# Self-attention over four images: first image's projection with its bias added on TensorE and one unit of lead, projection steps four ahead, column sums in a free PSUM bank, operands 64 bytes apart

## The chip, the cores and the metric

One core of a Trainium2 chip. TensorE (PE) multiplies, reading both operands from SBUF and writing sums into PSUM, which has eight banks of 128 x 512 float32 here. ScalarE (ACT), VectorE (DVE) and GpSimd (POOL) work beside it; SyncE (SP) and POOL issue most of the DMAs. Every engine works through its own queue in order, and semaphores hold an instruction back until what it reads or overwrites is ready. The metric is device time in microseconds (us) of one execution; lower is better.

## The reference

For each of four images, x has 4096 positions of 256 channels:

```
q = x @ Wq + bq          # 4096 x 128
k = x @ Wk + bk          # 4096 x 128
v = x @ Wv + bv          # 4096 x 256
pq, pk, pv = q, k, v reshaped to (-1, 4096)   # rows 128, 128, 256
energy = pq.T @ pk                            # 4096 x 4096
attention = softmax(energy, axis=-1)
out = pv @ attention.T                        # 256 x 4096, reshaped back
result = gamma * out + x                      # float32
```

## The kernel before, in words

**Number forms.** A float32 is kept as a shortened high part h and two combinations with the rest, so that products of the short type float32r add up to float32 accuracy. "Forms 0, 1, 2" are these three tensors: h is made by ACT (line 202 for x, 248 for q and k, 153 for v and the weights, 322 for the exponentials), the other two by DVE (204 and 206, 251, 156, 336 and 338). A product is built in one PSUM bank: first the products with form 2, then the partial sum is scaled in place (the "seed"), then the products with forms 0 and 1 are added on top.

**Projection.** An image has 16 units of 256 positions. One unit is: four transposes of x on PE (`transposed`, line 191), the forms of x (`x_forms`), q and k together (`products(b, i, 0, ...)`: 4 products of 128x256 with form 2, then 8 with forms 0 and 1), v (`products(b, i, 1, ...)`, likewise). Between the two parts stands the seed: for q and k on DVE, which scales by REST and adds the bias (`seed_qk`, line 233); for v on ACT, in two halves, with the bias as a column (`seed_v`, line 240). Then come the forms of the results; those of q and k go to DRAM in four stores of 192 KB on POOL's queue (`store`, line 270), from a tile with two buffers (`pf`). Image 0's v stays in SBUF (`vall`), the later images' v goes through DRAM as well.

Image 0 is projected alone ahead of everything (loop at line 527). In each iteration PE's order is: transposes of unit i+1, form-2 products of q/k of unit i, form-2 products of v, the rest of q/k, the rest of v. The first three query and key tiles are loaded in units 6 to 8 (lines 560 to 563), and the first two attention steps' scores are made in units 12 to 15. Six PSUM banks go round for all of it (line 515).

**Attention.** For each image there are 8 groups of 512 queries (g), and for each group 16 steps (t) of 256 keys: 128 steps an image, 512 in all (loop at line 567, n counts them). One step holds `cross` (2 products of 128x512 and ACT's scaling, lines 298 and 299), `energy` (4 products and ACT's exponentials, lines 313 and 316), both for two steps ahead (LOOK); `upper` (ACT's h of the exponentials); `halves` (DVE: running column sums at line 331 and the two other forms, for one step ahead); and `attend`, 12 products in two halves j of 6, into four PSUM banks a0, b0, a1, b1 (line 355). So a step has 18 products of 512 columns on PE. Into these steps the next image's projection is worked: `step(n, engine)` gives one eighth of a unit's work to each engine's place in a step (line 467), a unit in 8 steps, with r = step modulo 8 (0: transposes; 1 and 2: forms of x; 3: form-2 products of q/k and seed; 4: the rest of q/k; 5 and 6: v; 7 and 0: its forms). It uses two PSUM banks ("p", twice).

**Change of group.** At t = 15 and the following t = 0 the four banks are emptied into SBUF by ACT (`emptied`, line 369; j = 0 at t = 15, j = 1 at t = 0), and the column sums of the softmax are added over the partitions by two products with ones (`sum_forms`, lines 378 and 379, and `sums`, line 384), into bank b1 once that is emptied. ACT copies one row of it (line 385), and `finish` takes that row through DRAM to reciprocals, scales the group's output, adds x and stores it, some piece in each following step.

ACT's order around the change is: at t = 15 scalings, sum form, projection, exponentials, emptying j = 0, `upper`; at t = 0 scalings, emptying j = 1, projection, exponentials, the copy of the sums, `upper`. PE's order: at t = 15 `cross`, `attend` j = 0, `energy`, projection, `attend` j = 1; at t = 0 `cross`, `attend` j = 0, `energy`, `sums`, projection, `attend` j = 1. DVE makes its part of the sum form ahead of `halves`.

Of the kernel before, what the change touches and what calls it, by code (L numbers as in the profile page):

```python
# [20 lines left out]
def kernel(  # L21
# [36 lines left out]
    nc = tc.nc  # L58
# [42 lines left out]
    with ExitStack() as fast:  # L101
# [10 lines left out]
        ps_p = pool("ps_p", 2, space=PSUM)  # L112
# [4 lines left out]
        wf = qkv.tile([P, 2, 3, KC, C], F32R, tag="wf", name="wf")  # L117
# [8 lines left out]
        nc.gpsimd.memset(zs, 1.0)  # L126
        make_identity(nc, ident)
# [5 lines left out]
        nc.gpsimd.dma_start(gam, gamma.partition_broadcast(P))  # L133
        nc.gpsimd.dma_start(bias[:, :C2], bq.partition_broadcast(P))
        nc.gpsimd.dma_start(bias[:, C2:], bk.partition_broadcast(P))
        for eh in range(KC):
            nc.gpsimd.dma_start(bvs[:, eh : eh + 1], bv[eh * P : (eh + 1) * P].unsqueeze(1))
        nc.gpsimd.tensor_scalar(bias, bias, REST, None, ALU.mult)
# [20 lines left out]
        def weights(w):  # L159

            nc.scalar.mul(scaled[:, w], raw[:, w], E ** -(w + 1))
            yield from split(*(wf[:, w, f] for f in range(3)), scaled[:, w])
# [23 lines left out]
        def transposed(b, i):  # L186
            xs = loads.pop(("x", b, i))
            tp = units["xt", b, i] = bank(f"xt_{b}_{i}", [P, KC, 2, P])
            for k in range(KC):
                for s in range(2):  # L190
                    nc.tensor.transpose(tp[:, k, s, :], xs[:, s, k * P : (k + 1) * P], ident)  # L191

        def x_forms(b, i):

            y = units.pop(("xt", b, i))
            if b == 0:
                f = ppool.tile([P, 3, KC, 2, P], F32R, tag="ld", name=f"xf_{b}_{i}")
            else:
                f = work.tile([P, 3, KC, 2, P], F32R, tag="xf", name=f"xf_{b}_{i}", bufs=1)
            units["xf", b, i] = f  # L200
            h = f[:, 0]
            nc.scalar.activation(h, y, AF.Identity, scale=UPPER)  # L202
            yield
            nc.vector.scalar_tensor_tensor(f[:, 2], h.bitcast(F32), 1.0 + E, y, ALU.mult, ALU.subtract)
            yield
            nc.vector.tensor_tensor(f[:, 1], y, h.bitcast(F32), ALU.subtract)
            yield

        def products(b, i, w, fs):

            xf = units["xf", b, i]
            if fs[0] == 2:
                units[w, b, i] = bank(f"qv{w}_{b}_{i}", [P, 2, C])
            to = units[w, b, i]
            for f in fs:
                for s in range(2):
                    for k in range(KC):
                        if w:
                            left, right = wf[:, 1, f, k, s * P : (s + 1) * P], xf[:, f, k]
                        else:  # L220
                            left, right = xf[:, f, k, s, :], wf[:, 0, f, k]
                        nc.tensor.matmul(  # L222
                            to[:, s, :],
                            left,
                            right.rearrange("p s a -> p (s a)") if w else right,
                            start=(f == 2 and s == k == 0),
                            stop=(f == 1 and k == KC - 1),
                            skip_group_check=True,
                        )

        def seed_qk(b, i):
            y = units[0, b, i]
            nc.vector.scalar_tensor_tensor(  # L233
                y, y, REST, bias.unsqueeze(1).to_broadcast([P, 2, C]), ALU.mult, ALU.add
            )
# [137 lines left out]
        def sum_forms(n):  # L373

            s = now["total"] = now["sum"]
            f = work.tile([P, 2, NB], F32R, tag="r", name=f"zf_{n // NU}", bufs=1)
            h, l = now["z"] = f[:, 0, :], f[:, 1, :]
            nc.scalar.activation(h, s[:, 0, :], AF.Identity, scale=UPPER)  # L378
            nc.vector.tensor_tensor(l, s[:, 0, :], h.bitcast(F32), ALU.subtract)

        def sums(n):
            zp = ps_o.tile([P, NB], F32, tag="b1", name=f"z_{n // NU}")
            for f, x in enumerate(now["z"]):
                nc.tensor.matmul(zp, ones_r, x, start=(f == 0), stop=(f == 1))  # L384
            nc.scalar.copy(now["total"][0:1, 0, :], zp[0:1, :])  # L385
# [35 lines left out]
        def finish_last(n, xr):  # L421
# [26 lines left out]
            np_ = ps_p.tile([P, 1], F32, tag="p", name="np")  # L448
# [18 lines left out]
        def step(n, engine):  # L467
# [47 lines left out]
        now["banks"] = cycle(  # L515
            [(ps_o, "a0"), (ps_o, "a1"), (ps_o, "b0"), (ps_o, "b1"), (ps_p, "p"), (ps_p, "p")]
        )
        image(0)
        for i in range(3):
            load_x(0, i)  # L520
        transposed(0, 0)
        first = [weights(0), x_forms(0, 0), weights(1)]
        for pieces in first + [first[0], first[1], first[2]]:
            next(pieces)
        for pieces in first:
            next(pieces)
        for i in range(NI):
            load_x(0, i + 3)
            if i + 1 < NI:
                transposed(0, i + 1)  # L530
                xs = x_forms(0, i + 1)
            else:
                xs = iter(())
            products(0, i, 0, (2,))
            seed_qk(0, i)
            products(0, i, 1, (2,))
            next(xs, None)
            seed_v(0, i)
            if i in (12, 14):
                cross(i // 2 - 6)  # L540
# [4 lines left out]
            if i in (12, 14):  # L545
                energy(i // 2 - 6)
            vs = v_forms(0, i)
            next(vs)
            for _ in xs:
                pass  # L550
            for _ in qk:
                pass
            for _ in vs:
                pass
            store()
            if i in (13, 15):
                upper(i // 2 - 6)
            if i == 14:
# [5 lines left out]
            if i in (13, 15):  # L564
                load_k(i // 2 - 3)
        now["banks"] = cycle([(ps_p, "p")])
        for n in range(B * STEPS):
# [3 lines left out]
            if u == 0 and b + 1 < B:  # L571
                image(b + 1)
                load_x(b + 1, 0)
# [26 lines left out]
            attend(n, 1)  # L600
            if t == 6 and n + NU < B * STEPS:
# [221 lines left out]
```

## Time and profile before

| | |
|---|---|
| time, median of 3 runs | 2421.97 us (2421.1 to 2422.91) |
| the profiled execution | 2424.35 us, span 2422.6 us, granted clock 0.994 |
| busy: PE / DVE / ACT / POOL | 2358.6 / 2138.0 / 1870.8 / 581.7 us |
| projection of image 0 | from 0 to about 101 us, a unit from start to start mostly 5.03 us |
| a group of 16 steps with projection | 73.8 us (PE busy 73.2) |
| a group of 16 steps of the last image | 67.0 us |
| DMA moved | 413.8 MB, 170 GB/s of HBM traffic over the span |

The span runs from the first to the last instruction; the execution's time has some 1.75 us more around it. Busy times overlap between engines. PE's busy time includes the modelled end of each matmul, which overlaps the next one's start, so short waits of PE can lie hidden in it; distances from start to start show them. "Idle before" of an instruction is the time its engine did nothing, with the instruction that ended it. L233 is line 233 of the kernel.

### The profile page before, as it was taken

How to read it: one execution, taken by the hardware profiler on the slowest of the kernel's cores; microseconds unless marked ns; L12 is line 12 of the kernel's file. 1: busy time of each engine (PE TensorE's matmuls, PEld its weight loads, DVE VectorE, ACT ScalarE, POOL GpSimd, SP SyncE). 2: the span in 40 equal slices, each digit the busy share in tenths (PEclk: the TensorE clock that was granted, in tenths of full speed). 3: DMA queues.
4: the chain of work that ended last, by engine and by line, in shares of the span. 5: the costliest groups of instructions: out<-in, count | busy, mean ns of one | idle time of the engine just before them, and what ended most of it. 6: DMA issues, size and time to landing. Idle time of an engine off the chain costs nothing.

```text
span 2422.6 us, 31905 instructions
## 1 busy us (share of the span) xinstructions
PE 2358.6 (97%) x11094; PEld 1954.4 (81%) x11094; DVE 2138.0 (88%) x2126; ACT 1870.8 (77%) x3076; POOL 581.7 (24%) x943
## 2 busy tenths in 40 slices
PE   6799999999999999999999999999999999999998
PEld 6688888888888888888888888888888888888886
DVE  7789988889989899888899898898888888888887
ACT  4577777877877877778778778778777778787875
POOL 5422222222322222212233122222123111111110
PEclk9999999999999999999999999999999999999999
DMA  9756655656796666566699566675569644444443
GB/s 200 169 143 166 180 143 158 177 156 181 217 296 171 168 164 181 146 158 178 157 284 265 147 165 166 170 181 147 154 176 315 198 127 131 120 119 125 120 123 92
DMA packets 243990, 413.82 MB, mean 171 GB/s; under 512 B 26031, under 2 KB 141487, under 8 KB 243822
## 3 DMA queue, kind: packets, MB, share of 16 engines
q0 software_dynamic: 203152, 368.77, 57.2%
q1 hardware_dynamic: 40126, 42.67, 6.4%
q8 instruction: 91, 1.49, 0.3%
q14 instruction: 77, 0.63, 0.1%
q10 hardware_dynamic: 544, 0.26, 0.0%
HBM read 306.64 MB, written 104.98 MB: 170 GB/s over the span
## 4 chain that ended last, share of the span: by engine, by line
PE 86%; ACT 9%; DMA 2%; DVE 1%; issue 1%; POOL 0%; SPq 0%; DVEq 0%; ACTq 0%
PE a L355 35%; PE b L355 17%; PE e L313 17%; PE e L298 9%; PE qv L222 7%; ACT o L369 3%; ACT e L299 2%; ACT x L316 1%; ACT h L322 1%; PE z L384 1%; PE xt L191 1%; DMA k<-kf 1%; DMA qd<-f 1%; ACT zf L378 1%; DVE v L156 0%
## 5 line engine op out<-in xcount | busy, mean ns | idle before, releaser
L316 ACT ACTIVATE x<-e 128x512 f32<-128x512 f32 x960 | 523.8, 600 | 319.1 <-PE e L313 316.0
L285 POOL DMA_DIRECT2D k<-kf x512 | 275.8, 539 | 1743.3 <-PE e L313 1638.6
L331 DVE TENSOR_TENSOR s<-s,x 128x1024 f32<-128x1024 f32 x480 | 585.8, 1220 | 95.1 <-ACT x L316 92.7
L299 ACT ACTIVATE e<-e 128x512 f32<-128x512 f32 x1024 | 547.4, 574 | 137.2 <-PE e L298 136.5
L355 PE MATMUL a<-h,v 128*128 128x512 f32 x2048 | 640.0, 394 | 0.0
L355 PE MATMUL a<-ld,v 128*128 128x512 f32 x2048 | 633.4, 390 | 0.0
L355 PE MATMUL b<-ld,v 128*128 128x512 f32 x2048 | 631.7, 390 | 0.0
L336 DVE TENSOR_TENSOR ld<-x,h 128x1024 fp32r<-128x1024 f32 x480 | 585.4, 1220 | 30.9 <-PE b L355 24.8
L338 DVE SCALAR_TENSOR_TENSOR ld<-h,x 128x1024 fp32r<-128x1024 f32 x480 | 584.4, 1218 | 0.0
L313 PE MATMUL e<-q,k 128*128 128x512 f32 x2048 | 552.0, 391 | 4.5
L322 ACT ACTIVATE h<-x 128x1024 fp32r<-128x1024 f32 x480 | 509.9, 1062 | 13.3
L313 PEld LDWEIGHTS e<-q,k 128*128 128x128 f32 x2048 | 379.4, 188 | 98.1 <-ACT e L299 23.2
L355 PEld LDWEIGHTS a<-ld,v 128*128 128x128 f32 x2048 | 385.1, 188 | 83.2
L355 PEld LDWEIGHTS b<-ld,v 128*128 128x128 f32 x2048 | 383.9, 188 | 82.8 <-ACT s L385 1.4
L355 PEld LDWEIGHTS a<-h,v 128*128 128x128 f32 x2048 | 369.3, 189 | 62.7 <-issue 1.0
L298 PE MATMUL e<-q,k 128*128 128x512 f32 x1024 | 316.3, 390 | 0.6 <-DMA k<-kf 0.6
L298 PEld LDWEIGHTS e<-q,k 128*128 128x128 f32 x1024 | 192.0, 188 | 42.3 <-issue 1.6
L222 PE MATMUL qv<-wf,xf 128*128 128x256 f32 x768 | 117.6, 290 | 26.0 <-DVE qv L233 25.9
L222 PEld LDWEIGHTS qv<-wf,xf 128*128 128x128 f32 x768 | 109.1, 194 | 37.4 <-DVE qv L233 29.5
L222 PEld LDWEIGHTS qv<-xf,wf 128*128 128x128 f32 x768 | 108.8, 193 | 7.5
L222 PE MATMUL qv<-xf,wf 128*128 128x256 f32 x768 | 113.9, 285 | 0.0
L270 POOL DMA_DIRECT2D kf<-f x128 | 98.4, 769 | 41.0 <-ACT xf L202 20.6
(79 smaller groups left out, 1215.1 us busy)
## 6 DMA issues: line engine op xcount, KB each, us to landing
k<-kf POOLq DMA_DIRECT2D x512, 384.0 KB, 3.5
vf<-vf POOLq DMA_DIRECT2D x48, 768.0 KB, 6.0
v<-vf POOLq DMA_DIRECT2D x48, 768.0 KB, 7.2
kf<-f POOLq DMA_DIRECT2D x128, 192.0 KB, 3.4
qd<-f POOLq DMA_DIRECT2D x128, 192.0 KB, 3.1
q<-qd POOLq DMA_DIRECT2D x32, 768.0 KB, 4.7
o<-in_x_dram POOLq DMA_DIRECT2D x31, 512.0 KB, 7.7
out_dram<-o SPq DMA_DIRECT2D x31, 512.0 KB
```

The source lines that it names most:

```text
L222: nc.tensor.matmul(to[:, s, :], left, right.rearrange("p s a -> p (s a)") if w else right, start=(f == 2 and s == k == 0), stop=(f == 1 an ...
L270: nc.gpsimd.dma_start(to, f)
L285: nc.gpsimd.dma_start(t, kf[b, u % NU])
L298: nc.tensor.matmul(e, *forms(n, i, 2), start=True, stop=False, skip_group_check=True)
L299: nc.scalar.mul(e, e, -REST)
L313: nc.tensor.matmul(e, *forms(n, i, f), start=False, stop=(f == 1), skip_group_check=True)
L316: nc.scalar.activation(x[:, i, :], e, AF.Exp, scale=(1.0 + E) ** 3 / E)
L322: nc.scalar.activation(h, units[n], AF.Identity, scale=UPPER)
L331: nc.vector.tensor_tensor(s, s, x, ALU.add)
L336: nc.vector.tensor_tensor(l, x, h.bitcast(F32), ALU.subtract)
L338: nc.vector.scalar_tensor_tensor(d, h.bitcast(F32), 1.0 + E, x, ALU.mult, ALU.subtract)
L355: nc.tensor.matmul(to, vall[:, t, f, i, j * P : (j + 1) * P], units[n][f][:, i, :], start=(t == 0 and i == 0 and f != 1), stop=(t == NU - ...
```

## The change

- **Image 0's bias by PE.** q's and k's bias is split into two forms `bf`, divided by 128 (one made by ACT, one by DVE); four products of 128x256 with a matrix of ones add it into the bank behind the form-2 products (`biased`). The seed for image 0 is then a scaling alone, on ACT. The bias copies are issued first on POOL, gamma's last; POOL's scaling of `bias` for the later images moves behind the weights' forms.
- **A unit of lead.** In each iteration PE's order is: the rest of q/k of unit i, the rest of v, transposes of unit i+2, form-2 products and bias of q/k of unit i+1, form-2 products of v. Transposes alternate between the two p banks, products go round the four others. The loads of queries and keys move to units 4 to 6 (then 8 and 11), the first two steps' scores to units 7 to 12, `halves(0)` stays in unit 14.
- **Steps four ahead.** The projection's step is p = n for n < 8, two steps in each of n = 8 to 11, then p = n + 4. The next image's tiles and its first load are prepared five steps ahead of the image's end.
- **Change of group.** `sums` uses a p bank and stands behind the projection's products. At t = 15 `emptied` j = 0 stands where `upper` stood; `upper` follows at t = 0 behind the scalings; `emptied` j = 1 moves behind the exponentials of t = 0. DVE's part of the sum form moves behind `halves`.
- **64 bytes.** The tile of x's forms has 16 more elements at its start, and the weights' tile has the two sets exchanged with 32 elements between them, so that the two operands of a projection product no longer start at the same distance.

```diff
-        ps_p = pool("ps_p", 2, space=PSUM)
+        ps_p = pool("ps_p", 1, space=PSUM)
...
-        wf = qkv.tile([P, 2, 3, KC, C], F32R, tag="wf", name="wf")
+        wfs = qkv.tile([P, 6 * KC * C + 32], F32R, tag="wf", name="wf")
+        wf = [
+            wfs[:, o : o + 3 * KC * C].rearrange("p (f k c) -> p f k c", f=3, k=KC)
+            for o in (3 * KC * C + 32, 0)
+        ]
...
+        XF = 6 * C + 16
...
-        def bank(name, shape):
-            pool, tag = next(now["banks"])
+        def bank(name, shape, b, ring):
+            if b:
+                tile_ = spare(name, shape)
+                now["turn"] += 1
+                return tile_
+            pool, tag = next(rings[ring])
+            return pool.tile(shape, F32, tag=tag, name=name)
+
+        def spare(name, shape):
+            pool, tag = now["banks"][now["turn"] % len(now["banks"])]
             return pool.tile(shape, F32, tag=tag, name=name)
...
             if b == 0:
-                f = ppool.tile([P, 3, KC, 2, P], F32R, tag="ld", name=f"xf_{b}_{i}")
+                f = ppool.tile([P, XF], F32R, tag="ld", name=f"xf_{b}_{i}")
...
+            f = f[:, 16 : 16 + 6 * C].rearrange("p (f k s a) -> p f k s a", f=3, k=KC, s=2)
...
+        def biased(i):
+            to = units[0, 0, i]
+            for f in range(2):
+                for s in range(2):
+                    nc.tensor.matmul(
+                        to[:, s, :], ones_r, bf[:, f, :], start=False, stop=False,
+                        skip_group_check=True,
+                    )
...
         def seed_qk(b, i):
             y = units[0, b, i]
+            if b == 0:
+                nc.scalar.activation(y, y, AF.Identity, scale=REST)
+                return
...
             nc.scalar.activation(h, s[:, 0, :], AF.Identity, scale=UPPER)
+            yield
             nc.vector.tensor_tensor(l, s[:, 0, :], h.bitcast(F32), ALU.subtract)
+            yield
...
-            zp = ps_o.tile([P, NB], F32, tag="b1", name=f"z_{n // NU}")
+            zp = spare(f"z_{n // NU}", [P, NB])
...
+        products(0, 0, 0, (2,))
+        products(0, 0, 1, (2,))
+        biased(0)
+        seed_qk(0, 0)
+        seed_v(0, 0)
+        transposed(0, 1)
+        for _ in x_forms(0, 1):
+            pass
         for i in range(NI):
             products(0, i, 0, (0, 1))
             qk = qk_forms(0, i)
             next(qk)
             products(0, i, 1, (0, 1))
             vs = v_forms(0, i)
             next(vs)
+            xs = iter(())
+            if i + 2 < NI:
+                transposed(0, i + 2)
+                xs = x_forms(0, i + 2)
+                next(xs)
+            if i + 1 < NI:
+                products(0, i + 1, 0, (2,))
+                biased(i + 1)
+                seed_qk(0, i + 1)
+                products(0, i + 1, 1, (2,))
+                seed_v(0, i + 1)
+            load_x(0, i + 4)
+            for pieces in (qk, vs, xs):
+                for _ in pieces:
+                    pass
             store()
+            if i in (7, 10):
+                cross(i // 9)
+            elif i in (8, 11):
+                energy(i // 9)
+            elif i in (9, 12):
+                upper(i // 10)
+            elif i == 14:
                 halves(0)
-            if i == 6:
+            if i == 4:
                 load_q(0, 0)
-            if i in (6, 7, 8):
-                load_k(i - 6)
-            if i in (13, 15):
-                load_k(i // 2 - 3)
+            if i in (4, 5, 6):
+                load_k(i - 4)
+            elif i in (8, 11):
+                load_k(3 + i // 9)
         for n in range(B * STEPS):
...
+            if u == STEPS - 5 and b + 2 < B:
+                image(b + 2)
+                load_x(b + 2, 0)
...
             cross(n + LOOK)
+            turn = t == NU - 1 and not final
             if t == 0 and n:
-                emptied(n - 1, 1)
-            if t == NU - 1 and not final:
-                sum_forms(n)
-            step(n, "act")
+                upper(n + LOOK - 1)
+            if turn:
+                zf = sum_forms(n)
+                next(zf)
+            p = n if n < 8 else 2 * n - 8 if n < 12 else n + 4
+            step(p, "act")
             if not final:
                 attend(n, 0)
             energy(n + LOOK)
             load_k(n + LOOK + 3)
             store()
             if t == 0 and n:
+                emptied(n - 1, 1)
+            if turn:
+                emptied(n, 0)
+            else:
+                upper(n + LOOK)
+            step(p, "pe")
+            if t == 0 and n:
                 sums(n - 1)
                 active.append(finish(n // NU - 1, now["o"], now["total"]))
-            if t == NU - 1 and not final:
-                emptied(n, 0)
-            upper(n + LOOK)
-            step(n, "pe")
             halves(n + 1)
-            step(n, "dve")
+            if turn:
+                next(zf)
+            step(p, "dve")
...
             attend(n, 1)
+            if 8 <= n < 12:
+                for engine in ("act", "pe", "dve"):
+                    step(p + 1, engine)
```

More of the change, by code (lines that the diff above doesn't have):

```diff
@@ L161, in weights @@
             nc.scalar.mul(scaled[:, w], raw[:, w], E ** -(w + 1))
-            yield from split(*(wf[:, w, f] for f in range(3)), scaled[:, w])
+            yield from split(*(wf[w][:, f] for f in range(3)), scaled[:, w])
+        XF = 6 * C + 16
         def image(b):
@@ L212, in products @@
             if fs[0] == 2:
-                units[w, b, i] = bank(f"qv{w}_{b}_{i}", [P, 2, C])
+                units[w, b, i] = bank(f"qv{w}_{b}_{i}", [P, 2, C], b, 1)
             to = units[w, b, i]
@@ L514 @@
         now["made"] = {}
-        now["banks"] = cycle(
-            [(ps_o, "a0"), (ps_o, "a1"), (ps_o, "b0"), (ps_o, "b1"), (ps_p, "p"), (ps_p, "p")]
-        )
+        now["turn"], now["banks"] = 0, [(ps_p, "p0"), (ps_p, "p1")]
+        rings = cycle(now["banks"]), cycle([(ps_o, tag) for tag in ("a0", "a1", "b0", "b1")])
         image(0)
-        for i in range(3):
+        for i in range(4):
             load_x(0, i)
+        bf = work.tile([P, XF], F32R, tag="xf", name="bf", bufs=1)
+        bf = bf[:, : 2 * C].rearrange("p (f c) -> p f c", f=2)
         transposed(0, 0)
         first = [weights(0), x_forms(0, 0), weights(1)]
-        for pieces in first + [first[0], first[1], first[2]]:
+        for pieces in first + first:
             next(pieces)
+        nc.scalar.activation(bf[:, 0], bias, AF.Identity, scale=UPPER / P)
         for pieces in first:
             next(pieces)
-        for i in range(NI):
[L528 to L540, printed above, removed]
+        nc.vector.scalar_tensor_tensor(
+            bf[:, 1], bias, 1.0 / P, bf[:, 0].bitcast(F32), ALU.mult, ALU.subtract
+        )
+        nc.gpsimd.tensor_scalar(bias, bias, REST, None, ALU.mult)
+        products(0, 0, 0, (2,))
[6 more added lines that the diff above has]
+            pass
+        for i in range(NI):
             products(0, i, 0, (0, 1))
```

35 lines of the change are left out of this document (11 added, 24 removed).

## The prediction

> **What bounds the kernel now.** I read the busy table by stage first, then the engines' timeline of one unit of the first projection, the timeline around one change of query group, and last the waits. In the table the columns are the stretch, its length, busy time of PE, PE's weight loads, DVE, ACT and POOL with instruction counts, granted clock, DMA share and GB/s.
>
> ```profile
> 20.00:40.00 20.00, 14.15 (x113) 13.33 (x113) 16.98 (x29) 10.32 (x20) 12.37 (x17) 1.00 1.01 210
> 247.50:321.30 73.80, 73.20 (x347) 60.67 (x347) 66.51 (x67) 58.44 (x97) 17.50 (x29) 1.00 0.63 164
> ```
>
> The first projection leaves PE idle for 29% and no engine is full: a chain bounds it. The attention loop (one group of 16 steps, with two projection units of the next image) is PE's, but "busy" hides stalls, so I count starts. Now one unit (start, length, engine, line, what; in brackets the idle time before and what ended it); the next unit's first products start at 29.19:
>
> ```profile
> 24.15 1.22 PE L222 MATMUL qv<-wf,xf 128*128 128x256 f32 x8 [1.46 <-DVE qv L233]
> ...
> 25.21 1.12 PE L222 MATMUL qv<-xf,wf 128*128 128x256 f32 x8
> 25.41 0.60 ACT L248 ACTIVATE f<-qv 128x512 fp32r<-128x512 f32 x1 [1.76 <-PE qv L222]
> 26.04 1.28 DVE L251 SCALAR_TENSOR_TENSOR f<-f,qv 128x512 fp32r<-128x512 f32 x2 [0.76 <-ACT f L248]
> ...
> 26.17 0.60 PE L191 MATMUL xt<-ident,xs 128*128 128x128 f32 x4
> ...
> 27.24 1.28 DVE L156 SCALAR_TENSOR_TENSOR v<-v,qv 128x512 fp32r<-128x512 f32 x2
> ...
> 28.44 0.69 DVE L233 SCALAR_TENSOR_TENSOR qv<-qv,bias 128x512 f32<-128x512 f32 x1
> ```
>
> This is a closed ring: PE's last product, ACT's form (25.41), four DVE forms, the DVE seed (28.44) behind them in DVE's queue, and only then PE's next products. One turn is 5.04 us. Line 233 is what closes it.
>
> At a change of group:
>
> ```profile
> 174.72 1.08 ACT L322 ACTIVATE h<-x 128x1024 fp32r<-128x1024 f32 x1
> ...
> 175.67 1.10 ACT L299 ACTIVATE e<-e 128x512 f32<-128x512 f32 x2
> ...
> 176.34 1.21 PE L313 MATMUL e<-q,k 128*128 128x512 f32 x4
> ...
> 177.23 0.73 ACT L369 ACTIVATE o<-b,gam 128x512 f32<-128x512 f32 x1
> ...
> 178.01 0.73 PE L384 MATMUL z<-zf,ones 128*128 128x512 f32 x2 [0.45 <-ACT o L369]
> ...
> 178.94 0.71 PE L355 MATMUL a<-h,v 128*128 128x512 f32 x2
> ```
>
> PE's cross products of this step start at 174.22. To 178.94 PE does 14 products of 512 columns and 4 transposes. Away from the change two such products start 0.453 us apart (170.14 to 170.59), so 0.2265 each, and the transposes take 0.36: 3.53 us of work in 4.72. Some 0.03 to 0.09 of the difference follows every set of transposes, so a change costs **1.16 us**. It has two parts: line 313 is late because ACT ran an `upper` (174.72) ahead of the scalings (175.67), and line 384 waits until `b1` is emptied (177.23). The 31 changes cost about 36 us. The waits view (total us, times, longest) agrees in kind; it counts only idle time that no earlier product's modelled end covers:
>
> ```profile
> DVE zf L379 <- ACT zf L378: 97.2, 31, 3.3
> ...
> PEld z L384 <- ACT o L369: 27.5, 31, 0.9
> ...
> PEld e L313 <- ACT e L299: 23.2, 62, 0.6
> ```
>
> **The change, part by part.**
>
> *Start.* Bias copies now go out first on POOL; before they were issued at 2.15 and 2.69 and landed at 10.6 (5.8 and 7.9 us). The new first seed needs: landing, ACT form (0.6), DVE form (0.7), four bias products (at the half clock of this stretch 0.21 each), ACT seed (0.57) and some 0.1 of hand-overs, in all 2.9. With an unchanged landing P01 of unit 0 (the eight products of forms 0 and 1) starts at 13.5, with one 1.4 us earlier at 12.1; it was 13.69. I take the middle, 12.8.
>
> *One unit.* PE: 8+8 products at 0.12 (25.21 to 26.17 for eight) plus 0.1 for the first after a stall, 0.36 transposes, 4 products after them 0.56, 4 bias products 0.48. The bias product is not in this trace; its nearest row is the same 128x256 product. The last bias product starts 1.06+0.96+0.36+0.56+0.36, about 3.29 us into the unit, and ends 0.28 later; ACT's seed follows. Its form, PSUM to PSUM 128x512, is line 299's, 0.57. So P01 of the next unit starts after 3.29+0.28+0.04+0.57+0.03 = **4.21 us**. PE's own sum is 3.9, ACT's 0.5+0.5+0.5+0.53+0.93 = 2.96, DVE's six forms 6 x 0.61 = 3.7, POOL's four stores 4 x 0.78 = 3.1: all fit. The removed DVE seed bares nothing later than ACT's seed. Stores: issued 3.7 into the unit, landed 4.8 later (17.84 to 22.67), so at 8.5; the form buffer is wanted at 2 x 4.21+1.2 = 9.6. This leaves 1.1 of slack, where it had 2.8.
>
> Fifteen units from 13.69 to 97.22 took 83.5: 15 x 5.04 = 75.6 and 7.9 of special stalls. New: 15 x 4.21 = 63.2; half-clock start 0.9; unit 14 without transposes -0.4; energies and cross products of the early steps in units 7 to 11 (0.2 and 0.6 each, twice; `upper` hides in ACT's slack) 1.6, of which 0.6 falls into the next stall; and the load of q and k now at units 4 to 6. That load delayed stores by 4.5 before (55.34 landed at 62.44 instead of 57.8), and cost 3 us of waiting. With less slack, 1.1 and 0.9 a unit, following the queue unit by unit gives 2.4 + 0.5 + 0.5 = 3.3. Sum 68.0, so unit 15 starts at 80.8. The DVE forms of step 0 (`halves`, 2.3) no longer stand before a seed, which had cost 3.4 of the 7.9; now they delay unit 15's DVE forms, and step 0's first `b0` product, whose bank holds unit 15's q and k until those forms are read, waits 0.9, a product of step 1 0.3. From 80.8 PE has 1.06+0.96 of unit 15, then step 0 (0.45+1.36+0.9+0.91+0.36+1.36) and the cross products of step 1 (0.45): step 1's first attention product, at 107.0 before, comes at 88.6, and with the 0.3 the gain is **-18 us**. Ends: -11 if every unit takes 4.7, -22 if the load's stall vanishes.
>
> The bias as products costs PE nothing in the later images: only image 0 uses it.
>
> *Change of group.* Step p is now n+4, so at t=15 PE has 4 products of 256 columns, at t=0 eight. From the cross products of t=15 as zero: t=15 takes 4.55. ACT: scalings 0.43 to 1.45, sum form to 2.05, exponentials 2.46 (line 313's start plus 0.65, as at 182.23 and 182.88) to 3.5, `a0`, `b0` to 4.65; in t=0 scalings 4.98 to 6.0, `upper` to 6.95, exponentials 7.01 to 8.08, `a1` 8.08 to 8.78, `b1` to 9.3. PE in t=0: cross 4.55, attention 5.0 (`a0` free), energy 6.36 (scaled at 5.55 and 6.1, **no wait**), eight products 7.27, the sums 8.23 in a projection bank (no wait), attention at 8.68: it waits for `a1` 0.1, and 0.1 for the first product after a stall. So 0.23 of 1.16 is left. The displaced `upper` feeds DVE from 6.95 (forms at 9.25, used at 10.5 and later); the next `upper` and the copy of the sums sit behind the emptying until 10.75, and step t=1 has its scalings at 11.8 for an energy at 12.06. DVE's wait of 3.3 falls to 1.8, where it has room.
>
> This holds for 23 changes (n = 15 to 367). The last 8 have no projection: attention is reached at 7.25, `a1` is ready at 8.4, so 1.2 to 1.3 stays, and these gain nothing. **23 x 0.93 = -21 us.** Ends: 0 (the wait at `a1` eats all) and 31 x 1.16 = -36.
>
> *Four steps ahead.* The same instructions, earlier. Steps 8 to 11 carry two projection steps: PE 4.08+0.86, DVE 3.4+1.2, so PE still leads. At image ends the k load is waited for (PE 0.35 at 677.76, about 0.9 over three ends) and POOL waits 6.8 in all for v; both go: -1 (ends 0 and -2). x of image b+2 is issued one step ahead of its transposes, some 7 us, where the first x was there 3.3 us after its issue (0.72 to 4.06).
>
> *64 bytes.* In every run of 256-column products the starts lie 0.12 apart, whichever operand is loaded as weights and whichever buffer holds the forms; nothing in the trace ties it to an address. Half of a 512-column product would be 0.113, transposes go at 0.109, and a single gap of 0.125 occurs. So between -11 and +5 ns for 24 x 64 products, -17 to +8 us; I take **0**, the row that never varies. The Trainium skill (TensorE: Matmul & The Clock Gate, Part 2, step 1) says that weights and moving data come through two independent SBUF read ports, so that loading weights takes nothing from the running product: by that the offset is worth nothing, and the sum stays as it is. No row here separates the ports.
>
> *Sum.* -18 -21 -1 +0 = -40. The profiled execution took 2424.35 (span 2422.6 and 1.75 around it), 0.1% over the median 2421.97; so 2384 for such an execution, **2382** for the median.
>
> **Rivals.**
>
> *A, the offset pays.* Products at 0.113 instead of 0.120: 7 ns x 24 x 48 in PE's own stretches is 8 us, and about 2 in the first image: 2372 (2366 to 2376). For it: 0.120 is more than half of 0.2265. Against: the constancy. 17%.
>
> *B, the first image meets the DMA.* A store packet of 512 B takes 42 ns; 96 per engine and unit are 4.0 us, and the loads of q and k some 10.5 more in all. If these ran one after another, twelve units from the load on would take 12 x 4.0+10.5 = 58.5 instead of 12 x 4.21 and my 3.3 of stall, 53.8: 5 us more, 2387 (2384 to 2397). For it: a DMA share of 1.01 above. Against: packets overlap (a share of 1.52 and 351 GB/s in 56 to 60), and the engines stand empty in parts of 24 to 29. 15%.
>
> *C, a new wait at the change.* `a1` is emptied behind two exponentials; if ACT is 0.9 later than laid out, attention waits what the sums waited: 2403 (2395 to 2411). That is the case in which this part does not do what it says. For it: slack is -0.1; the last 8 changes show it in the sum above. Against: ACT's chain there has no other releaser. 10%.
>
> *D, slower: the offset hurts.* Each of the 1536 projection products reads operands that now lie 64 bytes apart. From 26 ns more each (0.146 instead of 0.120) this eats all 40 us; at 0.16 the time is 2382+61 = 2443. For it: no row shows such operands. Against: the largest gap in a steady run is 0.125. 4%; no visible change by some mixture 4%.
>
> The forecast itself has 50%, 2376 to 2388. The range to hold 8 in 10 takes in A and B and the nearer part of C: 2366 to 2400. About 0.2%, 5 us, is what a measurement here tells from no change: faster by that 0.92, within 0.04, slower 0.04.
>
> The clock: PE ran at half rate after idling 3.36 us (66.32: eight products in 2.07 instead of 1.22). My stalls stay at 2.4. The Trainium skill (same page, Part 1) puts the gate's window at about 3.4 us of idling; by that nothing is lost here, by a longer stall 1 to 2 us.
>
> **What would show it.** Right: in units 1 to 3 P01 starts 4.2 apart, released by ACT's seed; step 1's attention near 89; no wait at line 313 or the sums at a change, a small one at the first attention product with `a1` in the first 23, about 1.2 in the last 8; 256-column starts still 0.12 apart. Wrong: units near 4.9 with the form's write waiting for stores (B), group length still 73.8 (C), starts at 0.113 (A) or over 0.13 (D).

## The result and the profile after

The changed kernel takes 2417.82 us, median of 17 runs (2415.44 to 2419.44), beside 2421.03 us for the kernel before in 17 runs (2419.38 to 2424.64). The ratio is 0.9985, 95% interval 0.9978 to 0.9992: 3.2 us gained where 40 were forecast, and inside the 0.2% that the prediction called no change. The profiled execution took 2418.52 us (span 2416.6, granted clock 0.997).

In the table by stage (stretch, length, busy time and instructions of PE, PE's weight loads, DVE, ACT, POOL, then granted clock, DMA share, GB/s) the changed kernel shows the first projection, and one group of 16 steps, from a step's first attention product to that of 16 steps later:

```profile
20.00:40.00 20.00, 18.79 (x154) 17.80 (x152) 16.73 (x28) 14.43 (x29) 14.11 (x20) 1.00 1.21 234
237.80:311.50 73.70, 73.70 (x347) 60.78 (x346) 66.87 (x67) 58.61 (x96) 17.53 (x28) 1.00 0.63 165
```

The projection's stretch went from 113 to 154 instructions of PE in 20 us, transposes included. PE's busy time now fills the group. Yet the same 347 records take 73.7 us, where they took 73.8 with the waits of a change in them. Nothing waits more, so the instructions themselves take longer. On the page, two rows of the attention's products show it, first of before, then of after (last two numbers ahead of the idle time: busy us, mean ns of one):

```profile
L355 PE MATMUL a<-h,v 128*128 128x512 f32 x2048 | 640.0, 394 | 0.0
L355 PE MATMUL b<-ld,v 128*128 128x512 f32 x2048 | 631.7, 390 | 0.0
```

```profile
L382 PE MATMUL a<-h,v 128*128 128x512 f32 x2048 | 647.9, 397 | 6.6 <-ACT o L396 6.6
L382 PE MATMUL b<-ld,v 128*128 128x512 f32 x2048 | 638.3, 393 | 1.6 <-DVE f L278 1.6
```

The mean contains the modelled end, so starts are surer. Here is PE's timeline of one step of the last image, which has no projection, from `cross` to `cross` (18 products of 512 columns), before and after:

```profile
2313.28 0.61 PE L298 MATMUL e<-q,k 128*128 128x512 f32 x2
...
2317.36 0.61 PE L298 MATMUL e<-q,k 128*128 128x512 f32 x2
```

```profile
2310.43 0.62 PE L325 MATMUL e<-q,k 128*128 128x512 f32 x2
...
2314.59 0.62 PE L325 MATMUL e<-q,k 128*128 128x512 f32 x2
```

4.08 us against 4.16, without a wait in either. Over some 118 such steps the mean is 4080.6 ns before (226.7 for each product) and 4160.1 after (231.1). In the three images before it, whose steps hold a projection as well, the 512-column products that follow one another directly start 231.2 ns apart on average after. Before the change they started 227.9 ns apart there. Over all 512 steps that is tens of microseconds.

The parts that the change was about did come. In the first projection, the timeline of units 2 to 3:

```profile
18.20 0.58 ACT L258 ACTIVATE qv<-qv 128x512 f32<-128x512 f32 x1 [0.30 <-PE qv L250]
...
18.83 1.21 PE L236 MATMUL qv<-wf,xf 128*128 128x256 f32 x8 [0.20 <-ACT qv L258]
...
22.39 0.58 ACT L258 ACTIVATE qv<-qv 128x512 f32<-128x512 f32 x1 [0.30 <-PE qv L250]
...
23.02 0.38 PE L236 MATMUL qv<-wf,xf 128*128 128x256 f32 x1 [0.21 <-ACT qv L258]
```

A unit takes 4.19 us (18.83 to 23.02), released by ACT's seed; forecast was 4.21. And at a change of group, PE and ACT:

```profile
237.79 1.07 ACT L326 ACTIVATE e<-e 128x512 f32<-128x512 f32 x2 [0.34 <-PE e L325]
...
238.76 1.06 ACT L349 ACTIVATE h<-x 128x1024 fp32r<-128x1024 f32 x1
239.20 1.09 PE L340 MATMUL e<-q,k 128*128 128x512 f32 x4
...
241.05 0.62 PE L413 MATMUL z<-zf,ones 128*128 128x512 f32 x2
241.39 0.70 ACT L396 ACTIVATE o<-b,gam 128x512 f32<-128x512 f32 x1
241.57 0.73 PE L382 MATMUL a<-h,v 128*128 128x512 f32 x2
```

Neither the energies (239.20) nor the sums (241.05) wait. The attention behind the sums starts 0.52 after them, where two products take 0.46: 0.06 is left of 1.16.

From starts of single products: step 1's first attention product comes at 94.60 instead of 107.04 (12.4 gained), but from there to the first attention product of step 511 it takes 2303.4 us instead of 2296.3, 7.1 more. So something took back the whole gain of the changes of group, and 7 us besides.

### The profile page after: what moved, and what is told of

Its sections match the earlier page's. It is cut to its first block, busy times and chain, and to the rows that moved or that the text cites. A ratio compares the mean times of both kernels' runs of the same rounds, so it can differ in the third digit from the quotient of the medians.

```text
span 2416.6 us, 32018 instructions
## 1 busy us (share of the span) xinstructions
PE 2384.5 (99%) x11158; PEld 1964.7 (81%) x11158; DVE 2136.2 (88%) x2111; ACT 1882.9 (78%) x3093; POOL 582.3 (24%) x943
## 4 chain that ended last, share of the span: by engine, by line
PE 95%; ACT 2%; DMA 1%; DVE 1%; issue 0%; POOL 0%; SPq 0%; ACTq 0%; DVEq 0%; POOLq 0%
PE a L382 39%; PE b L382 19%; PE e L340 19%; PE e L325 10%; PE qv L236 7%; DMA qd<-f 1%; PE xt L204 1%; ACT x L343 1%; ACT o L396 1%; PE z L413 0%; ACT h L349 0%; ACT e L326 0%; DMA raw<-in_L_conv_Wv_dram 0%; DVE f L278 0%; PE qv L250 0%
## 5 line engine op out<-in xcount | busy, mean ns | idle before, releaser
L382 PE MATMUL a<-h,v 128*128 128x512 f32 x2048 | 647.9, 397 | 6.6 <-ACT o L396 6.6
L382 PE MATMUL a<-ld,v 128*128 128x512 f32 x2048 | 640.6, 394 | 0.0
L382 PE MATMUL b<-ld,v 128*128 128x512 f32 x2048 | 638.3, 393 | 1.6 <-DVE f L278 1.6
```

Source lines behind the costliest of these rows:

```text
L382: nc.tensor.matmul(to, vall[:, t, f, i, j * P : (j + 1) * P], units[n][f][:, i, :], start=(t == 0 and i == 0 and f != 1), stop=(t == NU - ...
```

## The experiments

Theory L: the 64 bytes did not act on the projection, but by enlarging two tiles. In the program as it is built, v, the weights, the halves, q, k and the forms of x all started at 256 bytes modulo 512 in their partition before. The change enlarged the weights' tile by 128 bytes and the forms' by 64, and tiles lie one behind another, so that v stayed at 256, the halves went to 384, q and k to 448. Weights and moving operand of an attention product now lie 128 bytes apart (modulo 512). Rival R1: PE, having lost its waits, is slowed by its own load. Rival R2: another part of the change slows the products.

**The change without its 64 bytes** (`e1_flush`):

```diff
-        wfs = qkv.tile([P, 6 * KC * C + 32], F32R, tag="wf", name="wf")
+        wfs = qkv.tile([P, 6 * KC * C + 0], F32R, tag="wf", name="wf")
...
-            for o in (3 * KC * C + 32, 0)
+            for o in (0, 3 * KC * C)
...
-        XF = 6 * C + 16
+        XF = 6 * C
...
-            f = f[:, 16 : 16 + 6 * C].rearrange("p (f k s a) -> p f k s a", f=3, k=KC, s=2)
+            f = f[:, : 6 * C].rearrange("p (f k s a) -> p f k s a", f=3, k=KC, s=2)
```

> The change without its 64 bytes: the two halves of the weights lie behind one another, the forms of x start at their tile's start, and every tile behind the weights keeps the address that it had before the change. Theory L (the 64 bytes moved every tile behind the weights, the halves, q, k and the forms of x, against the values of v, which stayed, and TensorE takes longer between two products with the operands so placed): the 512-column products go back from some 231.5 ns to 226.7 ns from start to start; over 9216 of them 41 to 44 us, so 2375 to 2381 us, ratio near 0.982. Rival R1 (TensorE, with fewer waits, is slowed by its own load): the pace stays near 231 ns and the time near 2418 us. Rival R2 (another part of the change, such as where the sums and units lie in PSUM, slows the products): the same, 2418 us.

Measured: 2383.63 us (4 runs), ratio 0.9855 (0.9838 to 0.9871). Its group and its step, in the same two views:

```profile
233.98:306.78 72.80, 72.80 (x347) 60.88 (x346) 66.82 (x67) 58.62 (x97) 17.48 (x28) 1.00 0.63 166
```

```profile
2269.72 0.62 PE L325 MATMUL e<-q,k 128*128 128x512 f32 x2
...
2273.80 0.62 PE L325 MATMUL e<-q,k 128*128 128x512 f32 x2
```

The same 347 records, PE just as busy, 0.9 us less for a group; a step is back at 4.08 us. R1 falls, since PE is as loaded here as after; R2 falls, since every other part is in. The 64 bytes cost 2417.8 - 2383.6 = 34 us.

Theory L expected more, 41 to 44 us, because it took the pace of the last image for all steps. From start to start, the 2304 products of the last image lose 4.4 ns each (226.7 to 231.1). The 6912 of the other images lose 3.4 (227.8 to 231.2), for in steps with a projection the pace is slower even without the 64 bytes. Together that is 10 + 23 = 33 us, close to the 34 of the times.

**The 64 bytes alone, on the kernel before** (`e2_bytes_alone`): the weights' and the forms' tiles as in the change, nothing else of it.

> The kernel before with only the 64 bytes of the change. L: every 512-column product takes 4 to 5 ns longer from start to start, 226.7 to some 231.5 ns, so 2421 + 41 = 2455 to 2465 us, slower. R1 (TensorE slowed by its own load, which here is as before): 2421 us, pace 226.7 ns. R2 (another part): 2421 us.

Measured: 2463.05 us (4 runs), ratio 1.0179 (1.0162 to 1.0196); a step of the last image 4186.8 ns. They cost 43 us there (2420.05 for the kernel before in the same series). The cost is larger than in the change, and so is the disorder: in this kernel the forms' tile stands between q and k, so q and the halves start at 384 and k at 448. The two operands of an energy product, equal in the change, lie 64 bytes apart here.

**Only a shift: no bytes inside the projection's operands, 128, 64 or 32 unused bytes behind the weights** (`e4_shift_only`, `e7_shift_64`, `e6_shift_32`); to the edit of the first run

```diff
-        wfs = qkv.tile([P, 6 * KC * C + 0], F32R, tag="wf", name="wf")
+        wfs = qkv.tile([P, 6 * KC * C + 32], F32R, tag="wf", name="wf")
```

and likewise with 16 and 8 elements.

> The change with the weights' halves and the forms of x where they were before (no 64 bytes between operands of the projection), but with 128 unused bytes behind the weights, so that halves, q, k and forms all lie 128 bytes further than before, as they do in the change. L: the attention's products, whose weights are the values of v (not moved) and whose moving operand are the halves (moved), lose 4 to 5 ns each, 6144 of them: 25 to 30 us over the run without the 64 bytes, and all of the 41 if the energies, whose q and k move together, are slowed too: 2403 to 2420 us. Rival L2 (what matters is the 64 bytes between the operands of one projection product, not the shift): 2375 to 2381 us. R1, R2: 2418 us, the same as without the shift.

> As the run with 128 unused bytes behind the weights, with 64 instead. L: the pace of the attention's products depends on the distance between weights and moving operand in some periodic way; it leaves 226.7 ns, to between 213 ns (the time of 512 columns at full rate) and 235 ns: 2330 to 2425 us; the likeliest is in between no shift and 128 bytes, near 2400 us. L2: 2375 to 2381 us. R1, R2: 2418 us.

> As the runs with 64 and 128 unused bytes behind the weights (2411.4 and 2422.4 us), with 32. Theory Lr with a smooth dependence on the distance: between no shift and 64 bytes, some 2395 to 2400 us, pace near 229 ns. Rival (any distance but a multiple of 512 bytes costs the same): 2411 to 2422 us. Rival (only distances of 64 bytes and more count): 2383 to 2386 us.

Measured: 2422.42, 2411.36 and 2427.69 us; a step of the last image 4173, 4134 and 4177 ns. So L2 falls: the shift alone costs 39, 28 and 44 us over the run without it, and the step of the last image, which holds no projection product, shows it. The time for 128 bytes lies 2 us above the range of L. The dependence on the distance is not smooth: 32 bytes cost the most, which none of the three theories for that run had foreseen.

**All operands shifted together** (`e9_all_shifted`): 128 unused bytes ahead of v.

> The change without its 64 bytes, with 128 unused bytes ahead of the values of v: now v, the weights, the halves, q, k and the forms all lie 128 bytes further, and no distance between two operands differs from the run without the 64 bytes (2383.6 us). Theory Lr (what counts is how weights and moving operand lie to each other): pace 227 to 228 ns, 2380 to 2387 us. Rival La (what counts is each operand's own address): as with the 128 bytes behind the weights or worse, pace 231 ns, 2415 to 2430 us.

Measured: 2385.96 us (4 runs), ratio 0.9852 (0.9837 to 0.9867); a step 4080.8 ns. For this shift it is the distance, not the address: La falls.

**The 64 bytes with everything else in its old relative place** (`e15_bytes_in_place`):

```diff
         ppool = pool("ppool", 2)
+        kpool = pool("kpool", 3)
         work = pool("work", 2)
-        kpool = pool("kpool", 3)
+        xpool = pool("xpool", 1)
...
-        vall = qkv.tile([P, NU, 3, 2, C], F32R, tag="v", name="v")
         wfs = qkv.tile([P, 6 * KC * C + 32], F32R, tag="wf", name="wf")
...
+        vall = qkv.tile([P, NU, 3, 2, C], F32R, tag="v", name="v")
```

with the later images' forms of x and `bf` from `xpool`, behind everything.

> The change with its 64 bytes (128 between the weights' halves, 64 ahead of the forms of x), but with the weights allocated ahead of v, q and k in another order and the forms of x last, so that v, the halves, q and k lie to each other as before the change, modulo 512 bytes. Theory Lr (the cost of the 64 bytes is all in the tiles that they moved): pace 227.5 ns, 2380 to 2386 us. Rival (the distance inside the projection's operands costs it too): 1536 projection products and the six 512-column ones behind each four or eight of them lose 1 to 5 ns: 2386 to 2395 us. Rival (the distance inside the projection pays, as its 256-column products were 1 ns nearer in the change): 2378 to 2382 us.

Measured: 2385.44 us (4 runs, 2381.78 to 2387.24), ratio 0.9854 (0.9837 to 0.9870). Its step:

```profile
2271.81 0.61 PE L326 MATMUL e<-q,k 128*128 128x512 f32 x2
...
2275.89 0.61 PE L326 MATMUL e<-q,k 128*128 128x512 f32 x2
```

4.08 again. The same bytes, with the tiles behind them in place, cost nothing that can be told from the run without them. The time alone does not separate the first rival from Lr, but the pace does: in the steps with a projection (32 to 352) the 512-column products start 227.6 ns apart here and 227.8 in the run without the bytes, so the distance inside the projection's operands does not slow them.

**The forms 64 bytes apart in the first image only** (`e10_forms_apart`): they start 64 bytes into a tile that has the room; nothing moves.

> The change without its 64 bytes, but the first image's forms of x begin 64 bytes into their tile, which has the room; nothing else moves. Only the 16 units of the first image have the two operands of a projection product 64 bytes apart. Theory L: a 256-column product there is bound by its own weight load of some 118 ns and not by its columns, so 0 to 0.1 us a unit either way, 2382 to 2386 us in all. Rival (spacing operands pays): starts 5 ns nearer, 24 products a unit, 2 us less: 2381 to 2382 us. Rival (spacing hurts here as it does for 512 columns): 5 ns more a product, 2 us more: 2385 to 2386 us.

Measured: 2384.44 us (5 runs, 2382.83 to 2387.95). The runs spread too far to tell the rivals apart. In the profiles an undisturbed unit takes 4.16 to 4.17 us instead of 4.23: 0.06 to 0.07, a size that L allowed, about 1 us for the image if every unit had it. The direction is the first rival's: the first image's products of 256 columns start 115.2 ns apart here, 119.6 in the run without the 64 bytes. They start closer than the 118 that L took for their bound. In the changed kernel it is 116.9.

**k alone, and q, k and the later forms together** (`e13_k_alone`, `e14_q_k_alone`): 128 unused bytes ahead of k, or ahead of all three; v and the halves stay.

> The change without its 64 bytes, with 128 unused bytes ahead of k alone, so that the 6 products of a step that take k as weights (the energies) lie 128 bytes otherwise to their moving operand q, and the 12 of the attention lie as in the run without the 64 bytes (2383.6 us). Theory Lr (each product pays for the distance between its operands): the 3072 energy products lose 4 to 5 ns, 12 to 15 us: 2395 to 2400 us, attention at 228 ns; if products behind a disturbed one are disturbed too, as those behind the projection are in the kernel before, up to 2415 us. Rival (only the attention's placing counts): 2383 to 2386 us.

> The change without its 64 bytes, with 128 unused bytes ahead of q, k and the later images' forms of x, all three moved together; v and the halves stay. Theory Lo (what counts is a product's own weights against its own moving operand): no such pair has moved but that of the projection, 2383 to 2390 us. Theory Ln (what counts is the weights that are loaded beside a running product, those of the next one, against the moving operand of the running one): in each step 4 products run beside a load of the other kind (from attention to energy and back, twice), 2048 products at 4 to 5 ns, 8 to 10 us: 2391 to 2394 us, and more, up to 2410, if the products behind them are disturbed too; the starts after the first product at such a place are 231 ns or more apart, those between two energy products 227.

Measured: 2423.48 us (a step 4167 ns) and 2407.30 us (4125 ns). Moving k alone cost 40 us, not 12 to 15. In the second run, no pair of an attention or energy product's own operands has moved, and it still loses 24 us: Lo falls. Its products tell where. Mean ns from a product's start to the next one's, in the order of a step of the last image (116 steps):

```
cross      231.0 232.4
attend j=0 231.0 227.4 227.4 226.8 226.9 232.6
energy     231.0 227.5 227.3 231.8
attend j=1 230.9 227.3 227.1 227.0 226.6 232.5
```

Where the kind changes, the last product of the old kind and the first of the new one take 4 to 6 ns longer; all others stay at 227. The last one runs while the weights of the new kind are loaded. That fits Ln. That the product behind it is late as well, at each place, is why the sum is some 45 ns a step and not 20. At a change of kind the moving operand's address steps by 128 bytes too, and this run alone cannot tell that step from the load beside it. The run with 128 bytes behind the weights can: from one of its attention products to the next the moving operand does not change its address modulo 512, only v lies 128 bytes away, and they take 228 to 241 ns. Its energy products, for which q and k moved alike, follow one another in 226.6 and 226.8 ns where neither neighbour is of the other kind. With k alone moved, even attention products whose own and next weights lie as before take 225 to 231 ns: a disturbance outlives its cause there by several products.

**The turn undone** (`e11_turn_undone`): the change without its 64 bytes, the loop over the steps as in the kernel before, with the sums in b1 and the projection not ahead.

> The change without its 64 bytes and without its new order at the change of group (order, the sums in b1, the projection's steps by the step's own number, as in the kernel before); the first image as changed. The turn forecast at 21 us, and read from the traces at 25 to 27: 2383.6 + 25 = 2405 to 2411 us, and the first attention product of step 1 still near 92. Rival (the first image's gain is lost later, and the turn gave it all): 2417 to 2421 us. Rival (the turn gave less than read, the gain coming from the first image): under 2400 us.

Measured: 2409.70 us (4 runs, 2406.45 to 2412.02). Its waits of PE's weight loads (total us, times, longest), then those of the change, which waits at the attention product instead:

```profile
PEld z L411 <- ACT o L396: 27.5, 31, 0.9
PEld e L340 <- ACT e L326: 23.3, 62, 0.6
```

```profile
PEld a L382 <- ACT o L396: 17.5, 31, 1.3
```

Against the run with the turn, the starts fall behind by 20.0 us in the 20 changes between steps 32 and 352, 1.00 a change, and by 0.09 a change in the last image. From step 1 to step 511 it is 23.7, and 26 by the times.

**The first image mended** (`e12_first_image`):

```diff
-        rings = cycle(now["banks"]), cycle([(ps_o, tag) for tag in ("a0", "a1", "b0", "b1")])
+        rings = cycle(now["banks"]), cycle([(ps_o, tag) for tag in ("a0", "b0", "a1", "b1")])
...
-            if i == 4:
-                load_q(0, 0)
-            if i in (4, 5, 6):
-                load_k(i - 4)
-            elif i in (8, 11):
-                load_k(3 + i // 9)
+            if 1 <= i <= NJ:
+                load_q(0, 0, i - 1)
+            if i in (5, 7, 9, 10, 12):
+                load_k((5, 7, 9, 10, 12).index(i))
```

> The change without its 64 bytes, with two edits in the first image: q is loaded in four parts, one in each of units 1 to 4, and the five loads of k are one to a unit at least, in units 5, 7, 9, 10 and 12, instead of q and three k in units 4 to 6; and the units take the banks in the order a0, b0, a1, b1, so that unit 15 holds a1 and b1 and not b0. Theory: the idle of TensorE at 44.4, 49.7 and 70.4 us (1.0 + 2.7 + 0.7 us over the usual step) comes from stores that stand behind the loads, and that at 86.9 (1.7 over) from b0 not yet emptied: with both gone step 1's first attention comes 5 to 6 us earlier and the time is 2377 to 2380 us. Rival (the loads take their time on the transfers wherever they are put): only the b0 wait goes, 2381 to 2383 us. Rival (the wait goes over to a1): the load stall alone goes, 2379 to 2381 us.

Measured: 2383.22 us (5 runs, 2382.61 to 2385.70), which the runs do not tell apart from 2383.63: the time forecast for it did not come. In its profile the parts show. PE at the place of the long wait, and at `b0`:

```profile
50.75 0.63 PE L329 MATMUL e<-q,k 128*128 128x512 f32 x2
51.22 1.12 PE L236 MATMUL qv<-wf,xf 128*128 128x256 f32 x8
...
89.33 0.63 PE L386 MATMUL a<-h,v 128*128 128x512 f32 x2
89.83 0.74 PE L386 MATMUL a<-ld,v 128*128 128x512 f32 x2
90.96 0.73 PE L386 MATMUL b<-ld,v 128*128 128x512 f32 x2 [0.40 <-DVE ld L369]
```

The wait behind `cross` is gone, and so is that at `b0` in step 0; step 1's first attention product comes at 89.33, 3.2 earlier, though this execution's first unit started 1.5 later (14.64 instead of 13.17). But step 1 now waits for its own half at `b0`, and from step 32 on the lead is 2.3. One execution each, and unit 0's start differs by more than a microsecond between executions; what the edit is worth in the time stays open.

Of all twelve, those with v, halves, q and k at the same address modulo 512 have a step of 4080 to 4081 ns; those with another placing have 4125 to 4187. The fastest kernels are the change without its 64 bytes, with or without the mended first image; each beats both the kernel before and the changed one.

## Why the prediction was wrong

**The step that failed is "64 bytes".** It took 0 from "the starts lie 0.12 apart, whichever operand is loaded as weights and whichever buffer holds the forms; nothing in the trace ties it to an address". Two errors stand in it. It priced 24 x 64 projection products, because the diff moves their operands; but a tile that grows moves every tile behind it, and the 9216 products of 512 columns were priced nowhere. And the row that never varies came from a kernel in which all these operands lay alike modulo 512: it held no other distance to show. A constant row bounds nothing outside the conditions under which it was taken. In the projection itself, whose operands came to lie 64 bytes apart for q and k and 192 for v, the cost is about 0, as was taken, or a small gain: 4.19 us a unit, beside 4.23 in the run without the bytes. In the attention loop it is +32 us in the profiled execution: the loop is 7.1 us longer than before, while without the bytes it was 25.0 shorter (2296.3 to 2271.3, step 1 to step 511). By the times it is 34.

Rival D named the right sign for the wrong products. Its condition, 26 ns on each of 1536, did not come; 3.4 to 4.4 ns on each of 9216 did. Rival A had the right sign for the projection: the starts came nearer, but only to 117 ns and not to 113.

The Trainium skill (TensorE: Matmul & The Clock Gate, Part 2, step 1) says that the moving operand and the weights have read ports of their own, so that a weight load takes nothing from the running product. By that the offset was worth nothing. The runs differ: in the run with q, k and the later forms moved, a product during which differently placed weights are loaded takes 232 to 233 ns from start to start instead of 227, and the one behind it 231. The measurement decides here; what in the reading or loading does this, no run shows.

**The change of group and the steps ahead** were forecast at 21 + 1 and measured at 23.7 in the profiles of the runs with and without the turn (26 by the times): 0.93 a change forecast, 1.00 measured, and almost nothing in the last eight, as forecast. Rival C did not occur.

**The first image** gained 12.4, not 18. This is one execution: in the profiles of the other runs with the same code for the first image, step 1's first attention product came at 91.4 to 95.9, a gain of 11 to 16. The unit of 4.21 was right (4.19 here, 4.23 without the 64 bytes); three sizes were off.
- *The load of q and k*, taken as 3.3 (its parts, 2.4 + 0.5 + 0.5, make 3.4). Units 6, 7 and 8 took 5.52 + 8.39 + 6.30 instead of 3 x 4.19; less 1.36 for the six early products of 512 columns, that is 6.3 us. ACT's write of the form waited 5.49 us for a store out of its buffer to land, and PE 3.93 behind it:

```profile
51.78 0.60 ACT L275 ACTIVATE f<-qv 128x512 fp32r<-128x512 f32 x1 [5.49 <-DMA qd<-f]
...
53.90 2.02 PE L236 MATMUL qv<-wf,xf 128*128 128x256 f32 x8 [3.93 <-ACT qv L258]
```

  That is rival B's releaser, inside B's range of sizes. With the loads spread (`e12_first_image`) the longest such wait was 2.7 us, which speaks for the loads as what lengthens it.
- *The clock*. The prediction let the stalls stay short. PE idled 3.93 us, and the table by stage shows the price in the granted clock (third number from the end), for the change, then for two runs with shorter and longer idling at the same place (`e1_flush` with 2.56 us, `e10_forms_apart` with 4.51):

```profile
53.89:60.00 6.11, 6.10 (x36) 5.97 (x37) 5.23 (x9) 4.38 (x10) 4.68 (x7) 0.72 0.90 170
```

```profile
52.70:57.51 4.81, 4.80 (x37) 4.63 (x37) 4.43 (x8) 4.49 (x10) 3.50 (x5) 1.00 1.09 239
```

```profile
55.04:62.00 6.96, 6.96 (x35) 6.88 (x36) 5.96 (x10) 4.41 (x9) 5.48 (x8) 0.60 0.86 175
```

  About 1.5 of the 6.3 are this: the unit behind the idling took 6.30 us, and 4.80 in `e1_flush`, whose clock stayed full. The three agree with the window of about 3.4 us that the Trainium skill gives (same page, Part 1).
- *Step 0's wait at `b0`*, taken as 0.9: PE's timeline has 2.18 between two pairs that take 0.46, so 1.7.

```profile
88.68 0.63 PE L382 MATMUL a<-ld,v 128*128 128x512 f32 x2
90.86 0.70 PE L382 MATMUL b<-ld,v 128*128 128x512 f32 x2 [1.55 <-DVE f L278]
```

The load (3.0 over), `b0` (0.8), unit 0 to unit 1 (5.68 instead of 5.1) and the start (13.15 instead of 12.8) make up 4.7 of the 6.0 us by which step 1 came later than forecast (94.60 instead of 88.6); the rest is in small pieces that were not followed.

Without its 64 bytes the change takes 2383.6 us, close to the 2382 forecast for the whole; but that closeness is partly luck. In its profile the first image gained 14.5 instead of 18 and the loop 25.0 instead of 22, and the two errors cancel. The kernel as changed does not reach it.

## What to carry to other kernels

A diff that enlarges a tile moves every tile behind it. List the addresses of all operands before and after, modulo 512 bytes here, and price every product whose moving operand lies otherwise to its own weights or to those of the next product, not only those that the diff names. When an engine is busy throughout and the time still grows, count instructions in a stretch of the same stage, and measure from start to start: 347 records in 73.7 us against 72.8 was the whole finding, with no wait to be seen.

## What the runs showed of the hardware

- With weights and moving operands at equal addresses modulo 512 bytes, products of 128x512 in float32r follow one another every 226.7 ns (4080.0 ns for 18). With distances of 32, 64 or 128 bytes, or a mixture, the mean over a step of the last image is 229 to 233 ns, and single positions take up to 241.
- It is the distance that counts: 128 bytes added to every operand cost nothing (2385.96 us beside 2383.63, a step of 4080.8 ns).
- Products of 256 columns are not slowed by it in the change: 118.5 ns before and 117.7 after in the later images. In the first image 119.6 ns at equal addresses became 116.9 in the change and 115.2 with the operands 64 bytes apart.
- Distances of 256 bytes and of less than 32 were not tried. So whether the pattern repeats every 512 bytes or oftener, and whether a placing exists that is better than 226.7 ns, stays open.
